# Four graph layers in one launch: the branch and its general arm moved behind the last store, the end of layer 3 rebuilt, three pieces one pair earlier

## The chip, the cores and the metric

The kernel runs on one core of a Trainium2 chip. The metric is the device time of one launch in microseconds (us); less is better. TensorE (PE) multiplies, with its weight loads shown as PEld; VectorE (DVE), ScalarE (ACT) and GpSimd (POOL) work element by element; SyncE (SP) issues most DMAs. Each engine takes its instructions in a fixed order. Between engines there are semaphores.

## The reference

There are 3327 nodes with 64 features each and a weighted, sparse 3327 x 3327 adjacency. Four layers follow each other, each of them `x = layernorm(x + layer(x, adj))`:

```python
# layer 0: mean over neighbours, beside the node itself
neigh = (adj @ x) / (adj.sum(1) + 1);   l0 = concat([x, neigh]) @ W.T
# layer 1: logarithm map between every pair of nodes (Poincare ball), weighted sum, exponential map
log_ij = logmap(x[:, None], x[None, :]); agg = einsum('ij,ijc->ic', adj / deg, log_ij)
l1 = expmap(0, agg @ weight + bias)
# layer 2: neighbours again, relu, each row divided by its norm
z = concat([x, (adj @ x + x) / deg]) @ W + b;  l2 = relu(z) / norm(relu(z))
# layer 3: of each row's neighbours the last 100 count, with weights that halve from the last one back
pos = rank - (deg - k);  w = mask * 0.5 ** (k - pos);  l3 = w @ (x @ weight) + bias
```

The final layernorm's result, 3327 x 64 float32, is the output.

## The kernel before

**Tiling.** The nodes are padded to 3328 = 26 blocks of 128. The columns of the transposed adjacency (the nodes that are being computed) are four chunks of 832; the rows (their neighbours) are 13 pairs of blocks. One load brings one pair for one chunk, 832 KB, into one of four buffers `adjp`. An accumulator is two PSUM banks' worth of half chunks (416 columns). PSUM has three double tiles (`two0` to `two2`, handed out by `banks.pair`) and two single ones (`one0`, `one1`, by `banks.one`).

**Layer 0** takes the chunks in the order 0, 3, 1, 2. It aggregates (L488) and on the way counts each row's neighbours for layer 3 (`count`, L560: rank bytes that ACT stores, L570). After each chunk `sums0` makes the sum of squares of its nodes; `features0`, which makes the layer's output from them, is put beside the next chunk's work, and for the last chunk beside the first steps of layer 1.

**The branch.** Layer 1 has two forms. `layer1_far` uses a short polynomial that is valid when no node lies near the origin of the ball; `layer1_near` is the general form. `sums0` marks near nodes in `near_nodes`; at the end of layer 0 the marks are summed (`nearest`, L796), summed over partitions by a small matmul (L798), and cast to an integer (`n_near`, L799). Each of the five engines loads this integer into a register (L1597) and branches (L1599). The far arm holds layers 1 to 3 in the far form; the near arm, behind it in every engine's program, holds layers 1 to 3 again with the general layer 1. With these inputs the far arm is taken. An instruction of an arm cannot stand ahead of the branch.

**Layer 1, far.** A step is one block of neighbours for one chunk, 104 in all. PE makes an inner product `v` (L858); DVE makes `p` from `v` and the adjacency (L869); ACT and POOL make the factor `s` (L882, L883, L884), or ACT and DVE do (L874, L877); six steps later PE aggregates with `s` (L889). Where an epilogue runs beside the steps, POOL has five of six factors, elsewhere every second one.

**Layer 2** takes the chunks in the order 2, 3, 1, 0: aggregation (L488) and an epilogue (`epilogue2`) that also writes `parts`, the operands of layer 3.

**Layer 3** sums `parts` with weights that are expanded from the rank bytes. A *piece* is one pair of blocks for one chunk. Its weights (`bits`) are made by ACT with an exponential (engine letter S, L1384), or by DVE and POOL (letter G: `exponents`, L1362, then L1380); the letters of the 52 pieces stand in `L3_ENGINES`. The first 18 pieces are put between pairs of layer 2 as `L3_AMONG` says: `{chunk turn: {pair: pieces}}`. Six pieces (`FILL3`, three for each of the chunks 0 and 3) use bf16 parts; the last 16 are the pairs 0 to 3 (`LATE3`) of chunks 2, 1, 0 and 3 in that order (`ORDER3`). Chunks 2 and 1 accumulate in double tiles, chunk 0 in the two single ones, chunk 3 in a double one.

After a chunk's last piece `keep_sums3` copies its two halves to SBUF (L1455), one on DVE and one on ACT. `epilogue3` multiplies with the weight (L1465), adds the residual (`y`, L1472, DVE), squares (L427, ACT), sums (L430, DVE), takes the inverse root of the variance and scales (`o`, L1488), and SP stores. The last chunk does this in two halves of 3 and 4 blocks. For the roots there is `deviation` (eight small DVE steps, L386 to L397) or, once ACT's root table is loaded (L1390, behind the last piece that ACT widens), `table_root` (one ACT lookup, L445, and three small DVE steps, L448 to L450).

The order on each engine is the order in which the code emits the work, changed by a scheduler where an instruction is not ready in its estimate; `issue_after(a, b)` fixes that `a` comes behind `b` on an engine.

Of the kernel before, what the change touches and what calls it, by code (L numbers as in the profile page):

```python
# [20 lines left out]
FP = mybir.dt.float32  # L21
# [5 lines left out]
AF = mybir.ActivationFunctionType  # L27
# [8 lines left out]
D = 64  # L36
# [80 lines left out]
L3_AMONG = {2: {5: 2, 8: 2, 12: 3}, 3: {1: 2, 3: 3, 8: 3, 10: 3}}  # L117


L3_ENGINES = "SSG" * 6 + "GSGSGS" + "S" * 12 + "SG" * 6 + "GSSG"  # L120
# [11 lines left out]
def four_gnn_layers_kernel(  # L132
# [109 lines left out]
    for t, value in ((minus_last, -1.0), (last_bias, 200.0)):  # L242
# [4 lines left out]
        )  # L247

# [430 lines left out]

    with ExitStack() as l0s:  # L680
        banks = Banks(l0s, "l0psum")
# [112 lines left out]
        count(masked, places, 0, counted)  # L794
        nearest = small.tile([P, 1], FP, name="nearest", tag="nearest")
        nc.vector.tensor_reduce(nearest, near, axis=AX.X, op=ALU.add)  # L796
        vote = banks.one(NCH % 2)
        nc.tensor.matmul(vote[0:1, 0:1], lhsT=nearest, rhs=ones, start=True, stop=True)  # L798
        nc.vector.tensor_copy(n_near, vote[0:1, 0:1])  # L799

    setup_stack.close()
# [31 lines left out]
    def layer1_far(banks):  # L845
        with tc.tile_pool(name="l1w", bufs=1) as wp:
# [109 lines left out]
            del work  # L956
            pairs = adj_pairs(first_pairs)
            waiting, last, side, total, summed, kept = [], None, None, NCH * NB, None, {}
            for start in range(0, total + L1_AHEAD, L1_GROUP):
                group = range(start, start + L1_GROUP)  # L960
                made = []
                for i in group:
                    if i < total:
# [5 lines left out]
                        v, v_issued = far_v(c, jb, summed)  # L969
# [3 lines left out]
                for i in group:  # L973
# [21 lines left out]

                    if late is None and i in (late_at, late_at + 2):
                        k0, k1 = (0, 4) if i == late_at else (4, GB)
                        transposes0(ORDER[-1], banks.one(1), v_issued, False, k0, k1)
# [23 lines left out]
            own = banks.pair()[:, 0, :]  # L1022
# [6 lines left out]
    def layer1_near():  # L1029
        with ExitStack() as stack:  # L1030
            all_of(features0(ORDER[-1], *last_group, Work(blocks_of(ORDER[-1])[2])))
            transposes0(ORDER[-1], Banks(stack, "l1b").pair())
# [184 lines left out]
    def begin2(banks, loading, loaded, behind):  # L1217
# [3 lines left out]
        rows = last_rows([(c, rank[:, c]) for c in ORDER2 if c != LATE_RANKS])  # L1221
        next(rows)
# [6 lines left out]
    def layers_2_and_3(banks, acc, done, rows, there):  # L1229


        with tc.tile_pool(name="l2m", bufs=M16) as mp, tc.tile_pool(name="late", bufs=1) as late:
# [86 lines left out]
            summed, split, loaded_all = [], [], []  # L1319
# [13 lines left out]
            def expand(behind=None):  # L1333
# [44 lines left out]
                for t, b in made:  # L1378
# [4 lines left out]
                    else:  # L1383
# [3 lines left out]
                        if k == last_widened and b != 0:  # L1387
                            done = t.bitcast(FP)
                            done = done[:, 1, 0:1] if len(t.shape) == 3 else done[:, 0:1]
                            nc.scalar.activation(nothing, done, AF.Abs_reciprocal_sqrt, bias=1.0)  # L1390
# [5 lines left out]
            def piece(k, behind=None):  # L1396
# [18 lines left out]
                if c not in acc3:  # L1415
                    if c == ORDER3[2]:
# [4 lines left out]
                bits, last = bits_of.pop(k), jp == LATE3[-1]  # L1421
                for b in range(2):
# [36 lines left out]
            def epilogue3(b0, b1_, bank, behind, made):  # L1459
# [11 lines left out]
                y = node_tile("y3")[:, 0:nb, :]  # L1471
# [4 lines left out]
                work = Work(nb)  # L1476
                ss = work("ss")
                held["adj"].append(-1)
                o = adjp.tile([P, 2, CH], FP, name="o", tag="adj").rearrange("p t c -> p (t c)")
# [174 lines left out]
```

## Time and profile before

| what | us |
|---|---|
| three runs | 514.81, 516.00, 516.71; median 516.0 |
| the profiled execution, whole time | 514.87 |
| its span, first to last instruction of the profile | 513.1 |
| so around the span | 1.8 |
| PE busy in the span | 470.9 (92%) |
| DVE, ACT, POOL busy | 388.5, 343.8, 210.0 |
| granted TensorE clock, mean | 0.987 |

The profile is one execution. A line of the timeline gives the start, the duration, the engine, the source line, what was done, and in brackets how long the engine had been idle and what ended that. Merged lines with `x4` run from the first start to the last end of four instructions. In the chain of waits a line gives start, length and what the end of the kernel was then waiting for. The windows view gives the busy time of each engine in a stretch. An engine name with a q (DVEq, SPq) is its sequencer, which loads registers, branches and issues DMAs.

### The profile page before, as it was taken

To read this page: it belongs to the slowest core of one execution; us is meant where nothing else is said; L and a number is where in the kernel's file an instruction comes from. 1 tells how busy PE (TensorE), PEld (TensorE's weight loads), DVE (VectorE), ACT (ScalarE), POOL (GpSimd) and SP (SyncE) were. 2 spreads that over 40 slices of the span, in tenths; PEclk is the share of its full clock that TensorE was granted. 3 is DMA by queue.
4 is the path that set the end of the run, shared out by engine and by line. 5 is a ranking of instruction groups with operands and counts; after the bars stand their busy time and mean duration, and the time that the engine had idled before them with its cause. 6 is when DMAs were issued, how large, how long until landed. Compare 5 with 4: busy or idle time off the path is not lost.

```text
span 513.1 us, 7873 instructions
## 1 busy us (share of the span) xinstructions
PE 470.9 (92%) x2888; PEld 239.7 (47%) x2888; DVE 388.5 (76%) x709; ACT 343.8 (67%) x430; POOL 210.0 (41%) x174
## 2 busy tenths in 40 slices
PE   5999999999966999999999999999999999899892
PEld 3444344454432333443443344354565555367782
DVE  3475429979849989889979987978787687637884
ACT  2445556686768988879968987820378746479862
POOL 2000201102118996769867986800412044310650
PEclk9999999999999999999999999999999999999996
DMA  8899999989729688867876788499779889950002
GB/s 273 293 387 329 391 388 371 320 291 307 264 78 341 220 265 269 256 200 263 265 246 220 243 271 258 164 343 399 264 242 361 294 317 333 303 225 2 0 1 74
DMA packets 46289, 132.49 MB, mean 258 GB/s; under 512 B 7046, under 2 KB 7150, under 8 KB 46178
## 3 DMA queue, kind: packets, MB, share of 16 engines
q1 hardware_dynamic: 45714, 131.36, 74.3%
q0 software_dynamic: 384, 0.52, 0.4%
q8 instruction: 24, 0.39, 0.3%
q14 instruction: 23, 0.19, 0.1%
q10 hardware_dynamic: 144, 0.03, 0.0%
HBM read 130.88 MB, written 0.85 MB: 257 GB/s over the span
## 4 chain that ended last, share of the span: by engine, by line
PE 49%; DVE 23%; DMA 12%; ACT 9%; issue 3%; POOL 2%; SPq 1%; DVEq 0%; POOLq 0%
DMA adj<-in_adjt_dram 12%; PE two L858 12%; PE one L889 11%; PE one L488 11%; PE two L560 4%; DVE mask L546 4%; PE two L488 4%; DVE mask L514 3%; ACT s L882 3%; ACT s L883 2%; DVE p L869 2%; PE two L1439 2%; DVE exponents L1362 2%; DVE s L877 2%; PE two L926 1%
## 5 line engine op out<-in xcount | busy, mean ns | idle before, releaser
L884 POOL TENSOR_TENSOR s<-s,p 128x832 f32<-128x832 f32 x70 | 135.5, 1955 | 34.6 <-DVE p L869 21.1
L869 DVE SCALAR_TENSOR_TENSOR p<-two,adj 128x832 f32<-128x832 f32 x100 | 101.6, 1019 | 15.1 <-issue 11.1
L570 ACT ACTIVATE rank<-two,last_bias 128x832 uint8<-128x832 f32 x78 | 71.8, 951 | 45.5 <-PE two L560 23.0
L858 PE MATMUL two<-uw 64*128 64x416 f32 x416 | 89.7, 544 | 8.7 <-DVE s L877 3.9
L889 PE MATMUL one<-s,xu 128*64 128x416 f32 x416 | 86.1, 525 | 0.0
L488 PE MATMUL one<-adj,x0w 128*64 128x416 f32 x416 | 82.9, 524 | 3.1 <-ACT x0w L698 1.8
L882 ACT ACTIVATE s<-two 128x832 f32<-128x832 f32 x70 | 60.0, 859 | 27.6 <-DVE p L869 27.1
L546 DVE SCALAR_TENSOR_TENSOR mask<-two,minus_last,mask 32x832 bf16<-32x832 f32 x48 | 52.5, 1093 | 30.8 <-PE two L560 27.5
L858 PEld LDWEIGHTS two<-uw 64*128 64x128 f32 x416 | 37.5, 189 | 60.6 <-PE one L889 16.9
L514 DVE TENSOR_SCALAR mask<-adj 128x1664 bf16<-128x1664 f32 x48 | 50.6, 1055 | 19.0 <-DMA adj<-in_adjt_dram 18.3
L883 ACT ACTIVATE s<-s 128x832 f32<-128x832 f32 x70 | 62.6, 897 | 1.8
L560 PE MATMUL two<-mask,tri 128*64 128x416 bf16 x416 | 52.3, 341 | 6.0 <-DVE mask L546 3.8
L488 PE MATMUL one<-adj,xr 128*64 128x416 f32 x264 | 54.1, 518 | 2.8 <-DMA adj<-in_adjt_dram 2.8
L889 PEld LDWEIGHTS one<-s,xu 128*64 128x64 f32 x416 | 26.0, 136 | 48.1 <-issue 41.7
L488 PEld LDWEIGHTS one<-adj,x0w 128*64 128x64 f32 x416 | 28.8, 138 | 35.5 <-issue 23.6
L1384 ACT ACTIVATE bits<-rank 128x832 fp32r<-128x832 uint8 (+1 forms) x42 | 38.8, 985 | 8.0 <-PE two L1439 6.0
L560 PEld LDWEIGHTS <-tri 128*64 128x64 bf16 x416 | 25.6, 110 | 38.4 <-issue 24.1
L1380 POOL TENSOR_SCALAR bits<-exponents 128x832 fp32r<-128x832 bf16 (+1 forms) x21 | 26.0, 1253 | 41.5 <-DVE exponents L1362 20.4
L877 DVE SCALAR_TENSOR_TENSOR s<-two,p 128x832 f32<-128x832 f32 x34 | 34.6, 1017 | 0.8 <-ACT two L874 0.3
L1439 PE MATMUL two<-bits,parts 128*128 128x416 f32 x144 | 30.9, 360 | 2.5 <-POOL bits L1380 2.3
L488 PEld LDWEIGHTS one<-adj,xr 128*64 128x64 f32 x264 | 20.8, 136 | 24.0 <-issue 15.9
L874 ACT ACTIVATE two<-two 128x832 f32<-128x832 f32 x34 | 28.8, 847 | 4.4 <-DVE p L869 3.6
(290 smaller groups left out, 540.3 us busy)
## 6 DMA issues: line engine op xcount, KB each, us to landing
adj<-in_adjt_dram SPq DMA_DIRECT2D x135, 832.0 KB, 5.6
uw<-in_adjt_dram SPq DMA_DIRECT2D x7, 832.0 KB, 6.2
a<-in_adjt_dram SPq DMA_DIRECT2D x8, 416.0 KB, 6.7
sums<-in_adjt_dram SPq DMA_DIRECT2D x2, 832.0 KB
p<-in_adjt_dram SPq DMA_DIRECT2D x4, 416.0 KB, 5.5
s<-in_adjt_dram SPq DMA_DIRECT2D x4, 416.0 KB, 6.8
uw<-in_xt_dram SPq DMA_DIRECT2D x1, 640.0 KB
out_dram<-o SPq DMA_DIRECT2D x2, 192.0 KB, 2.4
```

Of the source, the lines that this page charges most:

```text
L488: issued = nc.tensor.matmul(acc[h * D : (h + 1) * D, 0:HC], lhsT=x[:, 2 * jp + k, 0:D], rhs=a[:, bass.ts(h, HC)], start=(first and k == 1) ...
L514: issued = nc.vector.tensor_scalar(mask, a2, 0.0, None, op0=ALU.not_equal)
L546: ranks.carried = nc.vector.scalar_tensor_tensor(halves(last), ranks.after[P - 32 : P, :, 0:HC], minus_last[P - 32 : P, :], halves(last), ...
L560: issued = nc.tensor.matmul(counts[k][rows, h, 0:HC], lhsT=lhsT[:, rows], rhs=mask[:, of, bass.ts(h, HC)], start=lhsT is tri, stop=(k == 1 ...
L570: ranks.made = nc.scalar.activation(halves(ranks.rank[:, 2 * jp + k, :]), counts[k][:, :, 0:HC], AF.Relu, bias=last_bias,)
L858: issued = nc.tensor.matmul(v[:, h, 0:HC], lhsT=wt[rows, bass.ts(jb, P)], rhs=ut[rows, bass.ds(c * CH + h * HC, HC)], start=True, stop=True,)
L869: issued = nc.vector.scalar_tensor_tensor(halves(p), v, 0.25 - 0.5 * FD, halves(a), op0=ALU.add, op1=ALU.mult)
L877: return nc.vector.scalar_tensor_tensor(halves(s), v, FG, halves(p), op0=ALU.add, op1=ALU.mult)
L882: nc.scalar.activation(halves(s), v, AF.Square, bias=FB - 0.5, scale=-2.0)
L883: nc.scalar.activation(s, s, AF.Copy, bias=FG)
L884: nc.gpsimd.tensor_mul(s, s, p)
L889: issued = nc.tensor.matmul(acc[h * D : (h + 1) * D, 0:HC], lhsT=xu[:, jb, 0:D], rhs=s[:, bass.ts(h, HC)], start=first, stop=last,)
```

## The change

1. The far arm is no longer an arm. Layers 1 to 3 follow layer 0 straight, in the PSUM tiles of layer 0 (one set of `Banks` for all). PE's first `v` is ordered behind the last count.
2. The vote (`nearest`, the small matmul, `n_near`) stands at the end of layer 1, behind its last aggregation, in the second bank of the tile `own`.
3. The branch stands behind everything, as `tc.If(some_near > 0)` without an else. Its arm computes layers 1 to 3 again in the general form and stores over the output. It needs layer 0's output `xr`, which layer 1 overwrites, so POOL's queue writes it to HBM (`kept_x1`, 128 partitions of 6,656 bytes, 832 KB) when its last group is done; the arm reads it back. The arm doesn't repeat layer 3's `last_rows`.
4. In layer 2's last chunk three pieces stand behind pair 7 instead of pair 8.
5. The last piece of layer 3 goes from G to S, and so the table load moves behind this piece.
6. Chunk 3 accumulates in the two single tiles and chunk 0 in the double one; the fill pieces of chunk 3 come first. In chunk 3's last pieces the first half's matmuls end three matmul pairs ahead of the second half's.
7. Layer 3's epilogues of chunks 2, 1 and 0 stop after the sum of squares; their roots are finished later, with an ACT lookup and five small steps and the scaling on POOL. Chunks 2 and 1 are finished beside the last chunk's pieces, chunk 0 between the two halves of chunk 3. Those halves keep `table_root` and the scaling on DVE, in tiles of their own.

The diff, cut to its core:

```diff
-L3_AMONG = {2: {5: 2, 8: 2, 12: 3}, 3: {1: 2, 3: 3, 8: 3, 10: 3}}
+L3_AMONG = {2: {5: 2, 8: 2, 12: 3}, 3: {1: 2, 3: 3, 7: 3, 10: 3}}
-L3_ENGINES = "SSG" * 6 + "GSGSGS" + "S" * 12 + "SG" * 6 + "GSSG"
+L3_ENGINES = "SSG" * 6 + "GSGSGS" + "S" * 12 + "SG" * 6 + "GSSS"
...
+    kept = ctx.enter_context(tc.tile_pool(name="kept", bufs=1, space=bass.MemoryType.DRAM))
+    kept_x1 = kept.tile([P, NB, D], FP, name="kept_x1")
...
+    far = ExitStack()
+    banks = Banks(far, "psum_far")
     with ExitStack() as l0s:
-        banks = Banks(l0s, "l0psum")
...
-        count(masked, places, 0, counted)
+        counted = count(masked, places, 0, counted) or counted
+        banks.turns = [places.turn, 1, 2 - places.turn]
+    setup_stack.close()
+    def vote(bank, behind):
         nearest = small.tile([P, 1], FP, name="nearest", tag="nearest")
         nc.vector.tensor_reduce(nearest, near, axis=AX.X, op=ALU.add)
-        vote = banks.one(NCH % 2)
-        nc.tensor.matmul(vote[0:1, 0:1], lhsT=nearest, rhs=ones, start=True, stop=True)
-        nc.vector.tensor_copy(n_near, vote[0:1, 0:1])
-    setup_stack.close()
+        issue_after(nc.tensor.matmul(bank, lhsT=nearest, rhs=ones, start=True, stop=True), behind)
+        nc.vector.tensor_copy(n_near, bank)
...
-                        v, v_issued = far_v(c, jb, summed)
+                        v, v_issued = far_v(c, jb, summed or ahead_of)
...
+                    if late is None and i == late_at:
+                        nc.gpsimd.dma_start(out=kept_x1, in_=xr)
...
-            own = banks.pair()[:, 0, :]
+            own = banks.pair()
+            vote(own[0:1, 1, 0:1], summed)
+            own = own[:, 0, :]
...
     def layer1_near():
-        with ExitStack() as stack:
-            all_of(features0(ORDER[-1], *last_group, Work(blocks_of(ORDER[-1])[2])))
-            transposes0(ORDER[-1], Banks(stack, "l1b").pair())
+        nc.sync.dma_start(out=xr, in_=kept_x1)
...
-                    if c == ORDER3[2]:
+                    if c == ORDER3[3]:
                         acc3[c] = [banks.one(h) for h in range(2)]
...
+                if c == ORDER3[-1] and jp in LATE3:
+                    to_end.append((c, jp, bits))
+                    if len(to_end) < len(LATE3) - 1:
+                        turns3 = [(0, *to_end[-1]), (1, *to_end[-1])]
+                    elif len(to_end) == len(LATE3) - 1:
+                        turns3 = [(0, *to_end[-1])]
+                    else:
+                        turns3 = [(0, *to_end[-1]), (1, *to_end[-2]), (1, *to_end[-1])]
...
             def epilogue3(c, b0, b1_, bank, behind):
...
+                nc.scalar.activation(sq, y, AF.Square)
                 yield
-                if any(bank is last for c in ORDER3[1:] for last in acc3[c]):
-                    r, k = table_root(ss, work, made[-1]), -0.5 / D
+                nc.vector.tensor_reduce(ss, sq, axis=AX.X, op=ALU.add)
+                yield
+                if not ends_with:
+                    r, h = work("root"), work("part")
+                    issue_after(nc.scalar.activation(
+                        r, ss, AF.Abs_reciprocal_sqrt, bias=ln_eps, scale=1.0 / D
+                    ), tables[0])
+                    nc.gpsimd.tensor_scalar(h, ss, D * LN_EPS, -0.5 / D, op0=ALU.add, op1=ALU.mult)
+                    nc.gpsimd.tensor_mul(h, h, r)
+                    nc.gpsimd.tensor_mul(h, h, r)
+                    nc.gpsimd.tensor_scalar(h, h, 1.5, 1.0, op0=ALU.add, op1=ALU.mult)
+                    nc.gpsimd.tensor_mul(r, h, r)
+                    nc.gpsimd.tensor_tensor(o, y, col(r, nb), op=ALU.mult)
                 else:
-                    r, k = deviation(ss, work), 1.0
+                    r = table_root(ss, work, tables[0])
+                    nc.vector.scalar_tensor_tensor(
+                        o, y, -0.5 / D, col(r, nb), op0=ALU.mult, op1=ALU.mult
+                    )
...
-            pieces += [(c, jp) for c in ORDER3[2:] for jp in FILL3]
+            pieces += [(c, jp) for c in reversed(ORDER3[2:]) for jp in FILL3]
...
+                        for end in ends if tables and n < NCH else ():
+                            all_of(end)
+                        ends = [] if tables and n < NCH else ends
...
+                        if n == NCH:
+                            for turn3 in (1, 0, 2, 1, 0, 2):
+                                next(ends[turn3], None)
...
+    with far:
+        layers_2_and_3(banks, *layer1_far(banks))
     some_near = nc.values_load(n_near[0:1, 0:1], min_val=0, max_val=NP)
-    with tc.If(some_near == 0) as cmp:
-        with ExitStack() as arm:
-            banks = Banks(arm, "psum_far")
-            layers_2_and_3(banks, *layer1_far(banks))
-    with cmp.Else():
+    with tc.If(some_near > 0):
         done = layer1_near()
```

## The prediction

> **What bounds the kernel now.** I read the page first: which engine is full, and where.
>
> ```profile
> PE 470.9 (92%) x2888; PEld 239.7 (47%) x2888; DVE 388.5 (76%) x709; ACT 343.8 (67%) x430; POOL 210.0 (41%) x174
> ```
>
> PE sets the pace over the whole. The windows view says where it does:
>
> ```profile
> 146.00:152.00 6.00, 2.10 (x22) 1.33 (x22) 4.47 (x15) 3.55 (x5) 0.33 (x1) 0.96 0.45 142
> 152.00:174.00 22.00, 17.66 (x80) 6.91 (x80) 18.45 (x35) 17.32 (x22) 19.73 (x16) 0.93 0.88 284
> 186.00:338.00 152.00, 148.87 (x770) 61.96 (x770) 135.05 (x216) 124.11 (x156) 114.06 (x59) 1.00 0.73 241
> 500.00:513.00 13.00, 3.41 (x20) 2.94 (x18) 6.36 (x21) 2.64 (x7) 0.00 (x0) 0.62 0.29 73
> ```
>
> From 186 to 338 PE is full (152 / 770 = 0.197 us a matmul), and the windows up to 463 are nearly as full. So what comes earlier ahead of 186 stays earlier to the end. PE is empty in two places: at the join of layers 0 and 1, and after 500. The chain of waits shows the join:
>
> ```profile
> 150.15 0.18 DVE near_nodes L615
> 150.35 0.19 DVE nearest L796
> 150.58 0.20 PE one L798 x2
> 150.81 0.16 DVE n_near L799
> 150.97 0.99 issue
> 151.96 3.13 PE two L858 x8
> 155.12 1.03 DVE p L869
> ```
>
> The 0.99 us "issue" is the register load (0.48 to 0.54 us on each engine in the rows of the tile `n_near`), the branch and the waits behind it. The timeline of the end shows copies, matmuls and halves one after the other:
>
> ```profile
> 497.06 1.58 POOL L1380 TENSOR_SCALAR bits<-exponents 128x1664 fp32r<-128x1664 bf16 x1 [1.70 <-DVE part L391]
> ...
> 500.63 0.58 DVE L1455 COPY sums<-two 128x416 f32<-128x416 f32 x1
> ...
> 501.25 0.51 ACT L1455 COPY sums<-two 128x416 f32<-128x416 f32 x1 [2.90 <-DVE sums L1455]
> ...
> 503.20 1.97 PE L1465 MATMUL two<-w3s,sums 128*128 128x64 f32 x8 [0.52 <-DVE y L1472]
> ...
> 507.97 0.42 DVE L1488 SCALAR_TENSOR_TENSOR o<-y,root 128x256 f32<-128x256 f32 x1
> ```
>
> **The join: -3.6 us.** Without the vote DVE is done with `sums0` at 150.33 (150.15 + 0.17) and goes on to `p`, which now starts at 153.92. PE ends its last count at 147.99 and ACT its last rank store at 149.58, so the first two `v` are there before DVE is free. 153.92 - 150.33 = 3.6. The second pair of adjacency landed at 151.35 and is asked for two `p` later, at 152.4; SP can issue the third and later pairs from 147.2 instead of 151.71. At most PE's own lead counts, 151.96 - 147.99 = 4.0; at least 2.4, if DVE has to wait for ACT's last rank store and one full `v` and `p` (149.58 + 1.9 against 153.92). I take 3.6, since DVE is the last to come free.
>
> **`kept_x1`: +0.3.** One DMA issue on POOL. No transfer of 128 partitions from POOL is in the trace; its issues cost 0.51 (L585) to 1.77 us (L591, mean). POOL is full in 174 to 186 (12.00 of 12.00), but PE is too, and behind 186 POOL has 25% to spare. So 0 to 1.8, taken 0.3. Queued behind it on POOL are layer 1's factors. The 832 KB are one load more among 135; the DMA share is 0.81 in 174 to 186. SP's queue isn't passed.
>
> **The vote: +0.3.** A reduce of 0.18 and a cast of 0.15 on DVE, a matmul of 0.2 on PE at about 338.9, where own products (1.7 us) cover the copies of `sums`. Should the reduce stand behind the two L903 products (they end at 340.88) and the matmul ahead of the own products, PE waits 2.0 and the 28 matmuls behind it with it. 0 to 2.2; the reduce's input is ready since layer 0, so near the low end.
>
> **Three pieces a pair sooner: -1.4.** The row that carries it:
>
> ```profile
> 449.10 1.62 PE L488 MATMUL one<-adj,xr 128*64 128x416 f32 x8 [2.03 <-DMA adj<-in_adjt_dram]
> ```
>
> PE stands 2.03 us for pair 8's load. The three pieces (12 matmuls, 2.44 us) take that wait; their last weights were there at 446.79 (ACT, 445.90 + 0.89). Pair 8 then starts at 449.5, pairs 9 and 10 landed at 451.17 and 452.19, pairs 11 and 12 at 455.4 and 457.5 (+0.3, as pair 8's buffer comes free later). Pairs 9 and 10, the transposes (0.9), the next three pieces (2.4) and the last two pairs (3.0) end at 460.7 instead of 462.36, 1.6 sooner; 1.4 for small gaps. Behind it stands DVE's chain to `parts` (12.4 us, to 477.3), which starts everything after 478. At least 0, if weights come late, at most 2.0.
>
> **Layer 3's end: -2.4.** POOL's last weights end at 498.64 and PE's last piece at 499.72. As S the piece takes ACT 1.6 us (0.80 a half) behind its other weights (495.11), a square of 0.51 between: 497.2. But chunk 0's second copy and its 14 matmuls (1.8 us) wait in the same stretch, and then eight matmuls of pieces (1.4 to 2.1 us), so I leave PE's end at 499.7, -0.7 to +1.3. From there to DVE's last `o` it is 8.67 us now. With single tiles the copies stand side by side (0.63 instead of 2.0 us up to 501.76), DVE has no roots of other chunks ahead of its copy, and the second half's matmuls don't wait for `y`: 0.63 + 0.9 + 1.0 (matmuls of both halves) + 0.42 (`y`) + 0.42 (square) + 0.42 (sum) + 0.30 (root) + 0.6 (three steps) + 0.42 (`o`) + 0.24 (gaps) + 0.2 (chunk 0's `y` and sum between) = 5.6. That is -3.1. Against it: POOL's roots stand beside DVE. This row is the price:
>
> ```profile
> 157.93 1.94 DVE L436 SCALAR_TENSOR_TENSOR var<-ss_last,ln_eps 128x7 f32<-128x7 f32 x1
> ```
>
> A step that takes 0.17 us elsewhere took 1.94 beside POOL's L884 (157.91 to 159.86) and ended with it. Steps with an operand in PSUM (L374, 0.16) were not held. DVE's `part`, `root` and `o` lie wholly in SBUF; POOL's widest new operation is the scaling, 0.82 to 0.95 us (128x378 to 128x441). One such hold or several short ones: +0.7, from 0 to 2.9 (three scalings). Sum -2.4, from -4 to +1.
>
> The Trainium skill ("SBUF — State Buffer", Who interferes with whom) speaks here against the change: a VectorE instruction with two inputs in SBUF and a GpSimd instruction that reads SBUF cannot run together, and whichever starts first keeps the other out for its whole length. By that rule all three scalings could hold the last chain and the end would be worth -0.2 instead of -2.4; by the row it is only as much as happens to meet.
>
> **Costed at nothing:** the order of the fill pieces and the tiles that chunks 0 and 3 exchange. The matmuls are the same, and PE has them from 464.87 to 481.4 under DVE's chain to `parts`. If that cover went, the double tile, which DVE's epilogue leaves at 466.25, could hold chunk 0's fills for 1 us at most.
>
> **The branch at the end: +0.5.** SP's final stretch now: last store issued at 508.92, landed at 512.1, barrier to 513.06. Each engine already takes one far branch there: from its branch to its next instruction ACT needs 2.86 us (506.80 to 509.66), DVE 3.00 (507.98 to 510.98), SP 0.50. New is the register load, 0.54 on DVE: 511.5, still ahead of the landing. If SP must wait for its stores before the skipped arm and only then goes through its twelve final waits (0.06 each, 0.75), it costs 0.75 to 1.7. A second far branch would cost 3.0 on DVE, 2.4 of it visible. So 0 to 2.5; I take 0.5, as SP's row has 2.3 us of slack.
>
> **Sum.** -3.6 + 0.3 + 0.3 - 1.4 - 2.4 + 0.5 = -6.3. The profiled execution took 514.87 (span 513.1 and 1.8 around), which gives 508.6. It lies 1.1 under the median of the runs, so the forecast for the median is 516.0 - 6.3 = 509.7.
>
> **Rivals.**
> *The end gives nothing.* POOL holds DVE as in L436's row or ACT's longer row of weights, copies and roots delays chunk 0's copy. Then the end is worth +0.5 instead of -2.4: 512.6. For it: ACT's second copies waited 6.8 us in all for DVE's. Against: of these waits the last is removed by the single tiles.
> *The join was hidden.* In 152 to 174 POOL is 19.73 of 22 us busy, so the ramp has a limit of its own, and if POOL's extra DMA costs its 1.8 there and DMA or ACT hold the first steps, only 1 of 3.6 is left: 513.8, no change that can be told. Against: POOL's first factor (157.91) itself waits for the first `p`.
> *POOL's small steps set the end; slower.* POOL makes fifteen small steps and three scalings in a row, from about 498.0 (table load behind the last weights) minus the 5 gained: 493. No small two-operand step of POOL is in the trace. The line through 128x378 (0.818) and 128x441 (0.923) leaves 0.19 for none; the nearest row itself is 0.82, or 1.35 beside DVE (L612). With 0.2 each the three chunks take 5.9 and end at 499, ahead of DVE's end at 501.6 (508.4 - 3.6 + 0.6 - 1.4 - 2.4). From 0.4 a step they decide; at 1.2 each (18 + 2.9 us) chunk 0's store is issued at 514, and with 3.7 to land, 0.9 of barrier, 1.8 around and the median's 1.1 it is 521.5: slower. I take 0.2 from the line, since memsets of few elements take 0.09.
> *The end is worth all of its copies.* No hold, PE's end 0.7 sooner, no cost at the branch: 507.4.
>
> **How the numbers follow.** Forecast 0.60 (its own range 508.0 to 512.0), the end gives nothing 0.14, join hidden 0.08, POOL sets the end 0.10, the full end 0.08. The range 507.0 to 513.8 leaves out the slow case and the edges. About 0.5% (2.6 us) is what a measurement of this kernel can tell from no change, so faster means under 513.4: 0.60 + 0.12 + 0.08 = 0.80. Within it are the hidden join and the weak part of "gives nothing", 0.10; slower 0.10.
>
> **What would show it.** First `p` at 150.4 and layer 1's last aggregation at about 335.5 (338.9 now); no wait for a load at pair 8; chunk 3's two copies side by side; from PE's last piece to the last `o` 5.6 to 6.3 us instead of 8.7; POOL's small steps at 0.2 us; DVE's small steps at 0.17 unless POOL runs; between the last store's landing and the end at most 1.5 us. The forecast is wrong if `p` doesn't move, if POOL's scaling of chunk 0 ends behind DVE's last `o`, or if SP still works through waits long after the last landing.

## The result and the profile after

The changed kernel took 518.3 us (median of 22 runs, 515.3 to 522.5) against 515.4 us of the kernel before on the same chip: ratio 1.006, 95% interval 1.0037 to 1.0082. It is slower by about 3.1 us, where 6.3 us less was forecast, and it lies outside the range of 507.0 to 513.8. The profiled run happens to be its quickest (515.31 us, span 513.5); a second profile, further down, has a span of 517.5, nearer to the median.

The engines' line of the page and the windows that answer to those of before (columns: window, its length, busy us and count for PE, PEld, DVE, ACT and POOL, granted clock, DMA share, GB/s):

```profile
PE 473.0 (92%) x2888; PEld 239.9 (47%) x2888; DVE 381.6 (74%) x690; ACT 345.5 (67%) x432; POOL 215.2 (42%) x192
```

```profile
146.00:152.00 6.00, 5.34 (x47) 3.20 (x46) 3.76 (x10) 5.92 (x9) 0.00 (x0) 1.00 0.78 249
152.00:174.00 22.00, 17.09 (x82) 5.75 (x80) 19.88 (x42) 18.92 (x23) 17.04 (x11) 1.00 0.50 169
186.00:338.00 152.00, 148.20 (x768) 61.62 (x766) 134.71 (x213) 124.52 (x156) 114.24 (x59) 1.00 0.74 240
500.00:513.00 13.00, 3.32 (x28) 3.07 (x27) 5.15 (x15) 3.24 (x11) 4.99 (x16) 0.70 0.31 74
```

PE is no longer empty from 146 to 152, but not because layer 1 starts sooner: layer 0 ends later. Its last count ends at 152.07 (147.99 before). The join is 4.5 us shorter (first `p` 1.39 us after the last count instead of 5.93), so the first `p` comes at 153.46, 0.46 us sooner than before, and layer 1's last aggregation 0.8 us later than before. The rows, first of the kernel before, then of the changed one, where DVE takes the first `p` even ahead of the sum (L433) that belongs to `sums0`:

```profile
147.45 0.54 PE L560 MATMUL two<-mask,minus 128*64 128x416 bf16 x4
153.92 1.02 DVE L869 SCALAR_TENSOR_TENSOR p<-two,sums 128x832 f32<-128x832 f32 x1 [2.96 <-PE two L858]
```

```profile
151.53 0.54 PE L563 MATMUL two<-mask,minus 128*64 128x416 bf16 x4
153.46 1.02 DVE L866 SCALAR_TENSOR_TENSOR p<-two,sums 128x832 f32<-128x832 f32 x1
154.40 0.60 DVE L433 TENSOR_REDUCE ss_last<-sq 128x7 f32<-128x441 f32 x1
```

The join's gain is there; layer 0 had lost as much ahead of it. The timeline of GpSimd's queue shows what is new in layer 0, first of the changed kernel at its start:

```profile
4.19 0.79 POOL L585 MEMSET last_more<- 78x832 uint8 x1
4.92 0.09 POOL L727 MEMSET wl<- 1x1 f32 x1
4.96 1.75 POOL L587 DMA_DIRECT2D last_a<-in_adjt_dram  x3
```

and of the kernel before, where the same instructions stood behind the branch:

```profile
151.67 0.79 POOL L582 MEMSET last_more<- 78x832 uint8 x1 [20.88 <-DVE n_near L799]
152.41 0.73 POOL L584 DMA_DIRECT2D last_a<-in_adjt_dram  x1
153.14 0.51 POOL L585 DMA_DIRECT2D last_more<-rank  x1
```

Nothing in `last_rows` changed. But the three loads of `last_a` wait for no result, and with the branch gone nothing kept them back; the planner put them at 4.96 us. The DMA view of 2 to 20 us shows what they meet, first of the kernel before, then of the changed one (queue, packets, MB, share of the 16 engines):

```profile
q1 hardware_dynamic: 2312, 6.08, 99.8%
```

```profile
q1 hardware_dynamic: 1604, 5.39, 94.7%
q0 software_dynamic: 96, 0.26, 5.1%
```

SP's queue was full before (99.8%) and moves 0.69 MB less beside GpSimd's 0.26 MB. At 340 GB/s, the mean of that window before, 0.69 MB are 2.0 us, and DVE's fourth mask stands 1.9 us later (timelines of DVE, before and after):

```profile
16.03 1.03 DVE L514 TENSOR_SCALAR mask<-adj 128x1664 bf16<-128x1664 f32 x1 [0.51 <-DMA adj<-in_adjt_dram]
```

```profile
17.94 1.03 DVE L517 TENSOR_SCALAR mask<-adj 128x1664 bf16<-128x1664 f32 x1 [1.61 <-DMA adj<-in_adjt_dram]
```

In this profile PE then ran at half the clock from 20.6 to 27.5 us, and the 1.9 us had become 4.1 by the thirteenth mask. The windows of 20 to 42 us, before and after (the third number from the end is the clock):

```profile
20.00:42.00 22.00, 20.95 (x150) 10.66 (x148) 13.94 (x30) 9.14 (x13) 0.14 (x1) 1.00 0.93 329
```

```profile
20.00:42.00 22.00, 19.89 (x120) 9.87 (x122) 12.03 (x28) 9.33 (x13) 0.00 (x0) 0.84 0.88 290
```

The second new wait is at the vote. The changed kernel's timeline behind layer 1's last aggregation:

```profile
339.67 0.19 PE L809 MATMUL two<-ones,nearest 128*1 128x1 f32 x2
339.94 0.62 DVE L840 TENSOR_TENSOR xr<-one,vn 128x441 f32<-128x441 f32 x1
340.48 0.13 DVE L810 CAST n_near<-two 1x1 int32<-1x1 f32 x1
340.67 1.77 PE L909 MATMUL two<-w1r,uw 64*128 64x64 f32 x14 [0.81 <-DVE n_near L810]
```

The vote's result lies in the second half of the pair that the own products (L909) write. They wait for DVE's cast, and the cast waits behind `xr`: 0.81 us, with the matmul 1.0.

The pieces behind pair 7 do what was forecast. The wait for pair 8's load (2.03 us before) is gone; what is left is 0.32 us at pair 7:

```profile
448.00 1.62 PE L491 MATMUL one<-adj,xr 128*64 128x416 f32 x8 [0.32 <-DMA adj<-in_adjt_dram]
449.55 2.52 PE L1465 MATMUL two<-bits,parts 128*128 128x416 f32 x12
452.00 3.21 PE L491 MATMUL one<-adj,xr 128*64 128x416 f32 x16
```

The end, too, is much as forecast. Chunk 3's copies no longer wait for each other (DVE 499.73, ACT 501.66, each right behind its own half), GpSimd's small steps take 0.20 us, and from PE's last piece (501.62) to DVE's last `o` (507.03) it is 5.4 us, 8.7 before:

```profile
499.73 0.59 DVE L1481 COPY sums<-one 128x416 f32<-128x416 f32 x1 [2.24 <-PE one L1437]
501.19 0.43 PE L1437 MATMUL one<-bits,parts 128*128 128x416 f32 x1
501.66 0.51 ACT L1481 COPY sums<-one 128x416 f32<-128x416 f32 x1 [0.98 <-PE one L1437]
506.61 0.42 DVE L1541 SCALAR_TENSOR_TENSOR o<-sq,a 128x256 f32<-128x256 f32 x1
```

One DVE step met GpSimd's scaling of chunk 0:

```profile
505.42 0.94 POOL L1538 TENSOR_TENSOR o<-twice,root 128x448 f32<-128x448 f32 x1
505.48 0.89 DVE L452 TENSOR_TENSOR var<-var,a 128x4 f32<-128x4 f32 x1
506.41 0.16 DVE L453 SCALAR_TENSOR_TENSOR a<-var,a 128x4 f32<-128x4 f32 x1
```

A step of 0.16 us took 0.89: a hold of 0.73, as priced (0.7). Then the tail: from the last `o` to the end 6.5 us instead of 4.7.

### The profile page after: what moved, and what is told of

Read it like the earlier page. It is cut to its first block, busy times and chain, and to the rows that moved or that the text cites. A ratio compares the mean times of both kernels' runs of the same rounds, so it can differ in the third digit from the quotient of the medians.

```text
span 513.5 us, 7874 instructions
## 1 busy us (share of the span) xinstructions
PE 473.0 (92%) x2888; PEld 239.9 (47%) x2888; DVE 381.6 (74%) x690; ACT 345.5 (67%) x432; POOL 215.2 (42%) x192
## 4 chain that ended last, share of the span: by engine, by line
PE 53%; DVE 23%; DMA 9%; ACT 7%; issue 5%; POOL 2%; SPq 1%; POOLq 0%; DVEq 0%; ACTq 0%
PE one L491 14%; PE two L855 10%; PE one L886 9%; DMA adj<-in_adjt_dram 8%; PE two L563 5%; DVE p L866 4%; DVE mask L549 4%; PE two L491 4%; PE two L1465 3%; DVE mask L517 3%; ACT s L879 3%; DVE s L874 2%; ACT s L880 2%; DVE exponents L1364 2%; PE two L923 1%
## 5 line engine op out<-in xcount | busy, mean ns | idle before, releaser
L491 PE MATMUL one<-adj,x0w 128*64 128x416 f32 x416 | 85.3, 539 | 4.0 <-ACT x0w L702 2.6
L855 PEld LDWEIGHTS two<-uw 64*128 64x128 f32 x416 | 36.1, 185 | 61.8 <-issue 27.6
L563 PE MATMUL two<-mask,tri 128*64 128x416 bf16 x416 | 53.6, 346 | 5.6 <-DVE mask L549 3.9
L491 PE MATMUL one<-adj,xr 128*64 128x416 f32 x264 | 55.7, 518 | 0.8 <-DMA adj<-in_adjt_dram 0.8
L491 PEld LDWEIGHTS one<-adj,x0w 128*64 128x64 f32 x416 | 29.9, 142 | 37.3 <-issue 25.7
L1382 POOL TENSOR_SCALAR bits<-exponents 128x832 fp32r<-128x832 bf16 (+1 forms) x20 | 24.4, 1237 | 36.5 <-PE one L1465 19.3
L573 ACT ACTIVATE uw<-two,last_bias 128x832 uint8<-128x832 f32 x26 | 24.0, 951 | 12.2 <-DVE mask L549 6.1
```

The source lines that it names most:

```text
L491: issued = nc.tensor.matmul(acc[h * D : (h + 1) * D, 0:HC], lhsT=x[:, 2 * jp + k, 0:D], rhs=a[:, bass.ts(h, HC)], start=(first and k == 1) ...
L563: issued = nc.tensor.matmul(counts[k][rows, h, 0:HC], lhsT=lhsT[:, rows], rhs=mask[:, of, bass.ts(h, HC)], start=lhsT is tri, stop=(k == 1 ...
L573: ranks.made = nc.scalar.activation(halves(ranks.rank[:, 2 * jp + k, :]), counts[k][:, :, 0:HC], AF.Relu, bias=last_bias,)
L855: issued = nc.tensor.matmul(v[:, h, 0:HC], lhsT=wt[rows, bass.ts(jb, P)], rhs=ut[rows, bass.ds(c * CH + h * HC, HC)], start=True, stop=True,)
```

## The experiments

All ratios are to the kernel before, measured beside it; 0.001 is 0.52 us.

| kernel | median us | ratio (95% interval) | us |
|---|---|---|---|
| changed | 518.3 | 1.006 (1.0037 to 1.0082) | +3.1 |
| e1 changed, loads held | 515.6 | 1.0002 (0.9976 to 1.0027) | +0.1 |
| e2 before, loads early | 519.8 | 1.0084 (1.0061 to 1.0108) | +4.3 |
| e3 changed, no general arm | 517.2 | 1.003 (1.0003 to 1.0057) | +1.5 |
| e4 before, new end | 512.8 | 0.9964 (0.9939 to 0.9989) | -1.9 |
| e5 e1 and own bank | 511.3 | 0.9914 (0.9883 to 0.9945) | -4.4 |
| e6 e5 and chunk 0's store on ACT | 510.8 | 0.9902 (0.9874 to 0.9931) | -5.0 |
| e7 e4 and the pieces sooner | 512.3 | 0.994 (0.992 to 0.996) | -3.1 |
| e8 before, mended join alone | 514.1 | 0.9979 (0.9956 to 1.0002) | -1.1 |
| e9 e5 with the changed kernel's order | 513.8 | 0.9949 (0.9917 to 0.9981) | -2.6 |
| e10 changed, own bank alone | 514.2 | 0.9984 (0.9953 to 1.0015) | -0.8 |
| e11 e6 without the store of x1 | 510.4 | 0.9888 (0.9845 to 0.993) | -5.8 |
| e12 changed again | 518.6 | 1.0047 (1.0005 to 1.0089) | +2.4 |

**e1: the loads held.**

```
-        nc.gpsimd.memset(more, 200.0)
+        issued = [nc.gpsimd.memset(more, 200.0)]
...      (the loads of a and more are appended to issued)
+        for load in issued if hold is not None else ():
+            issue_after(load, hold)      # hold: layer 0's last count
```

> The changed kernel with the four kinds of GpSimd work of `last_rows` (the memset of `last_more`, the three loads of `last_a`, the three of `last_more`) put in GpSimd's order behind layer 0's last count, where the branch kept them before. Theory A (these loads, hoisted to 4.2 to 7 us, collide with the first adjacency loads): the fourth mask of layer 0 is back at about 16.0 us (17.9 in the changed kernel), layer 0's last count at about 148.0 (152.1), the first `p` at about 149.5 to 150.3 (153.5), and the time falls by 3 to 4.5 us, from 518.3 (median of the changed kernel) to 514 or less; against the kernel before 0.990 to 0.998. Rival B (layer 0 is late because of the clock, or because the new DRAM tile and the longer life of the PSUM pool moved something else): mask four and last count stay at 17.9 and 152, the time stays at 515 to 518. Rival C (the start is back, but the gain is given back at the join because GpSimd's loads now stand in the ramp): last count 148, first `p` 150, but the aggregation of layer 1 ends as late as now (339.7), time 517 to 518.

Measured: fourth mask 16.36, last count 147.28, first `p` 148.68, layer 1's last aggregation 334.96, 4.0 us sooner than before and within 0.6 of the prediction's 335.5. The edit orders the planner's list and makes no engine wait: in the profile the memset stands at 130.0 us and the first load at 131.6, the others behind the last count. So the loads are out of layer 0's start. Theory A holds for layer 0, and the time fell by 3.0 us, though to 515.6 and a ratio of 1.0002, not to the 514 or less that it asked for. And the lead was gone at the end of layer 2 (3.3 us later than before). So a second loss lies between 335 and 466 us.

**e2: the loads early in the kernel before.**

```
-            nc.gpsimd.dma_start(out=a[k * NB : (k + 1) * NB, :], in_=adjt[c, :, P - 1, :])
+            if len(chunks) == 1:
+                nc.gpsimd.dma_start(out=a[k * NB : (k + 1) * NB, :], in_=adjt[c, :, P - 1, :])
...
+    for k, c in enumerate(c for c in ORDER2 if c != LATE_RANKS):     # ahead of layer 0
+        nc.gpsimd.dma_start(out=last_a[k * NB : (k + 1) * NB, :], in_=adjt[c, :, P - 1, :])
```

> The kernel before with one thing added: the three loads of `last_a` for layer 2 are asked for on GpSimd's queue ahead of layer 0's first step instead of behind the branch; all else, the branch and the join too, is left. Theory A: layer 0's fourth mask at about 17.9 instead of 16.0 us, the last count at 150 to 152 instead of 148.0, and the time rises by 2 to 4.5 us, ratio 1.004 to 1.009. Rival B: nothing moves in layer 0, ratio 0.998 to 1.002 (the three loads that no longer stand behind the branch are worth under 1 us there, since GpSimd waits for the first `p`).

Measured: +4.3 us, theory A. With no other part of the change, the fourth mask stands at 18.14 and the last count at 149.88. The DMA view of 2 to 20 us is that of the changed kernel:

```profile
q1 hardware_dynamic: 1593, 5.36, 95.1%
q0 software_dynamic: 96, 0.26, 5.2%
```

Over all profiles, the last count ends at 151.1 us on average in the five with early loads (149.9 to 152.6) and at 148.0 in the nine others (147.2 to 149.4): 3.1 us, about what e1 gave back. Not all of e2's 4.3 us is lost in layer 0. In its profile the lag is 1.9 us from the first `p` to layer 1's last aggregation, 3.6 behind a half-clock window at 344.4 us, and 4.9 at layer 2's end. How much of that the loads set off and how much is the clock's spread is not shown.

**e3: no general arm.**

```
-    some_near = nc.values_load(n_near[0:1, 0:1], min_val=0, max_val=NP)
-    with tc.If(some_near > 0):
...
```

> The changed kernel without the register load, the branch and the general arm behind it (left out: the computation for near pairs, which these inputs do not need); the vote itself stays. Theory (the skipped arm makes SP wait for its stores queue by queue before the program's last waits): from DVE's last `o` to the end of the span 4.7 to 5.2 us instead of 6.4, time 1.2 to 1.8 us less than the changed kernel, 516.5 to 517.1. Rival (the tail is set by the order of the stores on SP behind GpSimd's chunk alone): the tail stays above 6 us and the time within 0.5 us of the changed kernel. Layer 0 should stay as late as in the changed kernel (fourth mask 17.9, last count 152).

Measured: 1.5 us less by the ratios, as expected; tail 5.56 us, more than the 4.7 to 5.2 expected; layer 0 as late as expected (18.98 and 152.64). Over all profiles the time from the end of the last store's issue to the end of the span is 3.8 to 4.1 us in the five that have no skipped arm there, and 4.5 to 5.0 in the seven that have one and keep all stores on SP. The arm costs 0.8 us in the tail: SP's twelve last waits (0.06 each) now begin only when the last store has landed. The rest of the tail is another matter, see e4 and e6.

**e4: the end alone.** The diff is that of the change for layer 3, without `L3_AMONG`, in the kernel before.

> The kernel before with the new end of layer 3 alone: the fill pieces in reversed order, the one-bank tiles for chunk 3, the last piece by ACT, GpSimd's roots for three chunks and the two halves side by side; the join, the branch and the pieces among pairs of layer 2 are as before. Theory (the profile of the changed kernel: DVE's last `o` came 2.7 us nearer to the end of layer 2, and the stores then went out behind GpSimd's chunk 0): last `o` 2.3 to 3.0 us sooner than before, end of span 1.7 to 2.7 us sooner, time 512.7 to 513.8, ratio 0.994 to 0.998. Rival (GpSimd's roots or the stores' order eat it all): ratio 0.999 to 1.003.

Measured: -1.9 us (interval -0.6 to -3.1), as expected. DVE's last `o` came 2.3 us sooner, but the tail is 6.4 us here too, with the branch at its old place. The rows of SP's stores say why: four stores now fall within 3 us, and the issue of one took 1.62 us instead of 0.37. In the profiles of e5, e7, e9, e10 and e12 one took 1.55 to 2.02. In the profile of before no store took more than 0.45. It does not happen every time: in the first profile of the changed kernel none took more than 0.48. There the tail's 1.8 us are 0.55 of later issue (three stores instead of two come behind the last `o`) and 1.2 behind the last issue, with the arm in it.

**e5: the vote in a bank of its own**, on top of e1.

```
-            own = banks.pair()
-            vote(own[0:1, 1, 0:1], summed)
-            own = own[:, 0, :]
+            own = banks.pair()[:, 0, :]
+            vote(banks.one(NCH % 2)[0:1, 0:1], summed)
```

> The first experiment's kernel (loads held behind layer 0) with the vote's matmul in a PSUM bank of its own instead of the second half of the own products' pair. With it the planner's order of DVE in layer 2's second chunk is again that of the kernel before. Theory A: no 0.81 us wait of PE for `n_near`; from layer 1's last aggregation to layer 2's first 3.4 to 3.7 us (4.3 in the changed kernel, 3.3 before), the 2.75 us or so that the second chunk of layer 2 lost between 384 and 398 us falls to that of before; together 1.6 to 2.2 us less than the first experiment, 513.3 to 514. Theory B (the clock gate: after short idle times of PE whole windows of 3.4 us run at half the clock, 1.7 us of matmul time each; the first experiment had one pair of them at 337.3 right behind the wait for the vote and one at 432.9): with the waits gone the median of the granted clock rises to 0.986 or more and the time falls by 3 us or more, 512.5 or less. Rival C: neither matters, 515 to 516.

Measured: 4.5 us less than e1 by the ratios, well over the 1.6 to 2.2 of theory A. Its timeline:

```profile
337.46 0.19 PE L809 MATMUL one<-ones,nearest 128*1 128x1 f32 x2
337.58 0.43 PE L909 MATMUL two<-w1r,uw 64*128 64x64 f32 x2
337.91 0.14 DVE L810 CAST n_near<-one 1x1 int32<-1x1 f32 x1
337.94 1.78 PE L923 MATMUL two<-wl,sums 128*128 128x66 f32 x14
```

The vote now stands among the own products and nobody waits for the cast. The time is in theory B's range (512.5 or less), but its sign, a higher clock, is missing: the median is 0.985 in e1 and 0.9845 here. So neither theory is right as it stands. What did change besides the wait is the order that the planner gives DVE in layer 2 from 384 to 398 us; e9 takes that alone.

**e9: that order alone.**

```
                         x2, based = prologue2(c, issued)
+                        if n == 1:
+                            issue_after(summed[-1], based)
```

> The kernel of the run with the own bank (511.3) with one order added: DVE's sum `ss` of layer 2's first chunk is put behind `twice` of the second chunk's `prologue2`, which gives DVE between 384 and 398 us the order of the changed kernel, with no wait for the vote. Theory A (of the 4.2 us between the first experiment and the run with the own bank, the larger part is this order: PE waits 1.4 to 1.9 us for `sums` ahead of the second chunk's `wl` products where the others wait 0 to 0.6, and the ranks' tail is later): 512.3 to 514.0, 1 to 2.7 us more than with the own bank, PE's wait for `sums` back at 1.2 us or more. Rival B (the order costs nothing that lasts; the difference is the wait for the vote and half-clock windows that it sets off): 511.0 to 511.8.

Measured: 1.8 us more than e5 by the ratios, 2.4 by the medians; the intervals of the two overlap. The order is nearly that of the changed kernel (`ss` stands behind the last step of `twice`, there behind the first). The wait is there. PE's waits from 380 to 437 us, in the changed kernel:

```profile
PE two L1269 <- DVE sums L474: 1.4, 1, 1.4
```

and from 330 to 437 us in e9 and e12 alike:

```profile
PE two L1269 <- DVE sums L474: 1.9, 1, 1.9
```

Before, it was 0.6 us (L1267), e6 and e11 have 0.3 and 0.7, and e5, e8 and e10 show no such line. In e9's profile the lead over the kernel before is 2.1 us at layer 2's 312th aggregation matmul of 416 and a lag of 2.2 at the 320th. Not all of these 4.3 us belong to the order: beside the wait for `sums` PE waits 1.1 us for `parts`, and a half-clock window (430.5 to 433.9 us) falls there. The first profile of the changed kernel, without such a window, loses 0.7 between the same two matmuls. So e9 shows that the order brings the wait; the 1.8 us are its price only in part. In this order DVE takes `ss` of the first chunk behind `twice` of the second, and the root, `xu`, `parts` and the last masks of the ranks follow later: in the changed kernel's profile `xu` and `parts` by 2.8 us and the last masks by 1.0 to 1.9, counted against the masks ahead of them.

**e10: the own bank alone.**

> The changed kernel with the vote in a bank of its own and nothing else changed; the early loads of `last_rows` stay. If the two causes add: 518.3 - 4.2 = 514.1, from 513.4 to 515, layer 0 still late (last count 150 to 152.6). If the bank's effect was an accident of the first experiment's planning: 516.5 to 518.

Measured (the edit of e5 on the changed kernel): 514.2 us, 3.9 us less than the changed kernel by the ratios. The two causes add: 3.0 (loads) and 3.9 (bank) make 6.9, and e5, with both mended, lies 7.5 below the changed kernel.

**e6: chunk 0's store on ACT's queue**, on top of e5.

```
+                if c == ORDER3[2]:
+                    yield
-                nc.sync.dma_start(
+                stored = (nc.scalar if c == ORDER3[2] else nc.sync).dma_start(
...
+                if c == ORDER3[2]:
+                    issue_after(stored, tables[-1])      # DVE's last o
```

> The same with one more change: the store of chunk 0 (GpSimd's) goes out on ScalarE's queue behind ScalarE's last root, so that SP's stores of the last chunk do not stand behind it. Theory: SP's last store is issued 0.5 us after DVE's last `o` instead of 1.1, the end of the span 5.6 to 6.0 us after the last `o` (6.4 in the changed kernel), 0.4 to 0.8 us less than the run with the own bank; 512.6 to 513.5, under the kernel before. Rival: ScalarE, later at its far branch by the store (2.7 us from branch to the next instruction), ends the program: tail 6.4 or more, no gain.

Measured: 0.6 us less than e5, less than the intervals can tell. The half of the expectation about the issue holds, the half about the tail does not. SP's last store is issued 0.46 us after the last `o`, and none takes long, but the tail is 6.8 us: it lands later, 4.6 us after its issue (3.2 before). The rival's reason doesn't hold either: ScalarE is through with its waits at 508.0 us, SP with the last store at 508.8. With this the kernel is faster than the kernel before and the changed one, 0.9902 (0.9874 to 0.9931).

**e7: end and pieces**, without the rest (`3: {1: 2, 3: 3, 7: 3, 10: 3}` in e4).

> The kernel before with the new end of layer 3 and the three pieces a pair sooner, the join and the branch as before: the fourth experiment plus the pieces. Theory: the pieces are worth 1.2 to 1.4 us as the profile of the changed kernel has it (pair 8 waits 0.5 instead of 2.0 us for its load), 511.4 to 511.6 where the end alone had 512.8; ratio 0.991 to 0.994. Rival: the wait for the loads comes back two pairs later and the gain is under 0.4.

Measured: 1.2 us less than e4 by the ratios, 0.5 by the medians. From the end of pair 7 to layer 2's end its profile takes 13.9 us, that of before 15.3 and that of the changed kernel 14.1; neither waits at pair 8.

**e8: the mended join alone**, layer 3's end and the pieces as before, loads held, own bank.

> The kernel before with the new join alone: branch and general arm behind the last store, `kept_x1`, the vote behind layer 1 in a bank of its own, `last_rows`' loads held behind layer 0's last count; layer 3's end and the pieces as before. Theory A (the join's gain holds): the first `p` at 148.7 to 149.5, layer 1's last aggregation 3.7 to 4.2 us sooner than before (338.95), layer 2's end 3 us or more sooner, the tail 0.9 us longer: 512.5 to 513.2, ratio 0.993 to 0.996. Rival B (the join's idle time was a rest that the clock gate gave back elsewhere, or layer 2's loads, at 0.9 to 1.0 of the DMA engines' time from 335 to 360 us, set the pace there): layer 1 ends 4 us sooner, but layer 2 at most 1.5 us sooner, time 514.5 to 516, ratio 0.998 to 1.001.

Measured: -1.1 us (interval -2.3 to +0.1), between the two theories. In its profile the first `p` follows the last count by 1.40 us (5.93 before). The last count itself stands 1.1 us later, so the lead is 3.4 us at the first `p`; 2.1 of it are left at layer 1's end, 2.6 at layer 2's, and 1.9 at the end of the span.

**e11: no store of x1** (the saved x1 for the general arm is left out).

> The kernel with all mended (510.8) without the store of `kept_x1` (the saved x1 for the general arm is left out; these inputs do not read it). The prediction set +0.3 for it, within 0 to 1.8. If it is 0.3 or less: 510.2 to 511.0, and layer 1's ramp loses 0.5 to 0.7 us of the join's lead between the first `p` and the 52nd aggregation as with the store. If the store is what takes the ramp's lead: 509.5 or less and the lead at the 52nd aggregation is within 0.2 us of that at the first `p`.

Measured: 0.4 us less by the medians, 0.7 by the ratios, within what the intervals leave open. The lead shrinks from 4.9 us (first `p`) to 4.3 (52nd of layer 1's 416 aggregation matmuls) without the store too (4.6 to 4.0 with it), so the ramp's loss is not the store's.

**e12: the changed kernel again.**

> The changed kernel again, for a second profile beside its fastest one. Expected: 517.5 to 519; layer 0's fourth mask at 17.9 to 19.0 us and its last count 1.9 to 4.7 us behind that of before (1.9 if no window of half clock falls into the start, 4 or more if one or two do); PE's wait for the vote 0.8 us; PE's wait for `sums` ahead of the second chunk's products 1.2 to 1.9 us; and one or two more windows of half clock than the first profile.

Measured: 518.6 us; fourth mask 18.28 us, last count 1.9 us late with no half-clock window at the start, the vote's wait 0.8 us, the wait for `sums` 1.9 us. Not as expected, the half-clock windows are not more than in the first profile: two, now at 340.8 us, where they cost 3.3 us (from layer 1's last aggregation to layer 2's 52nd the lag grows by 4.3 us, in the first profile by 1.0). And one store's issue took 2.02 us, for a tail of 7.7 us (6.5 in the first profile).

## Why the prediction was wrong, point by point

**The join, -3.6: the gain is there, the step was not complete.** The first `p` moved to within 1.4 us of the last count, 5.9 before. That is 4.5 us, more than the 4.0 given at most, since the sum assumed that `p` comes behind all of `sums0`. With the loads held it stands at 148.6 to 150.8, where 150.3 was forecast. The step that failed is its list of what can move ahead once the branch is gone: it asked what SP can issue sooner (pairs 3 and later) and what PE and DVE can start, but not GpSimd. A branch holds back every instruction behind it on every engine. The prediction quoted GpSimd's row of loads (L585, 0.51 us) as a price and did not ask where the loads go. They went 147 us ahead, into a stretch in which SP's queue was 99.8% of the DMA engines' time. Cost: 3.0 us in e1's return, 4.3 in e2; directly seen are the 1.9 us of the fourth mask.

**The vote, +0.3: mis-sized, 3.9.** The prediction weighed one bad case, the reduce behind L903, with 2.0 us. The wait came by another way: the tile. The diff puts the vote into the pair of the own products, so the work named as its cover waits for it. The profile shows 1.0 us for this. e9 puts 1.8 us more on the order of DVE in layer 2, which the planner chose once the vote stood there; that price is uncertain, as said at e9. Where the remaining 1.1 us go stays open. The median clock is 0.982 in the changed kernel and 0.9845 in e10, by estimate 1.3 us of 515, so they may lie in the clock.

**"What comes earlier ahead of 186 stays earlier to the end": too strong.** It holds roughly: of e1's and e6's lead at the first `p` (5.2 and 4.6) 4.0 and 3.4 are left at layer 1's end. The losses are short, counted in layer 1's 416 aggregation matmuls: 0.6 to 0.7 us up to the 52nd (1.8 in e5, with a half-clock stretch from 155.6 us), then 0.35 us between the 104th and 156th in every kernel with the new join, and 0.2 between the 260th and 312th in all of them but e11, which has no store of x1. Join, vote, store and branch were to give -2.5 together; e8 measured -1.1.

**Three pieces a pair sooner, -1.4: about right** (-1.2 by the ratios of e7 and e4, whose intervals overlap; 1.4 and 1.2 behind pair 7 in the profiles of e7 and of the changed kernel).

**Layer 3's end, -2.4: right in mechanism and near in size** (-1.9, e4). The steps of its sum show in the timeline: copies that don't wait for each other, one hold of 0.73 us, small steps of 0.20 us. The rival in which GpSimd's small steps set the end falls by that 0.20. The cost was in what the prediction placed under the branch: the stores crowd on SP.

On the skill's rule there ("SBUF — State Buffer", Who interferes with whom): of GpSimd's three scalings only the last was running when a DVE step with two SBUF inputs was due, and it held that step to its end (to 506.38 against 506.36), as the rule has it. DVE's reductions and its steps with a PSUM operand ran at 0.34 to 0.62 us beside the other two.

**The branch at the end, +0.5:** 0.8 in the tails of the profiles, its low case of 0.75. Unforeseen was the issue of 1.5 to 2.0 us among crowded stores.

**The sum.** Forecast -6.3, measured +3.1; no rival named either of the two causes. Of the 9.4 us, 3.0 are the loads, 3.9 the vote's bank (e10), 1.4 the join with the store, the branch and the mended vote (e8 against -2.5), 0.5 the end and 0.2 the pieces; 0.4 are left, less than the intervals. Mended in these two places the kernel takes 511.3 (e5), -4.4 us, inside the range that was given for the change.

## What to carry to other kernels

A branch, or any barrier, is also a fence for work that depends on nothing: before taking one out, list every instruction behind it, engine by engine, that has no producer (memsets, loads), and ask into which stretch it will rise; if that stretch is bound by the same resource, tie it down. A result of one element costs its wait, not its size: look at which tile it lands in, and who writes the rest of that tile next. When a small wait is added under a planner, the order of later work can change too, so compare the engines' order well past the edit.

## What the runs showed of the hardware

From 2 to 20 us 0.26 MB of GpSimd's loads displaced 0.69 MB on SP's queue, with the DMA engines at 1.01 of their time in both (340 and 316 GB/s); why more than byte for byte is open.

Stores in quick succession on one queue: 0.37 us an issue becomes 1.55 to 2.02 for one of them in the profiles of e4, e5, e7, e9, e10 and e12, not in those of the changed kernel, e1 and e3 (0.48 to 0.63 at most).

Half-clock stretches of 3.41 us, or 6.83, fall into full stretches of PE. The windows of e6, the middle one cut at the clock's own edges:

```profile
335.70:339.18 3.48, 3.48 (x30) 3.25 (x30) 1.83 (x5) 0.94 (x2) 0.00 (x0) 1.00 1.02 397
339.18:342.59 3.41, 3.41 (x11) 1.24 (x12) 2.85 (x6) 0.15 (x1) 0.00 (x0) 0.50 1.03 413
342.59:346.00 3.41, 3.41 (x22) 1.41 (x20) 2.37 (x12) 0.60 (x2) 0.00 (x0) 1.00 1.03 405
```

Eleven matmuls instead of 22 in the middle one, so 1.7 us lost, although PE was busy for all of the window ahead of it, with 64- and 66-column matmuls. e1, e5, e11 and e12 have such a window near there, and so does e2 with the old join; the profile of before and the first of the changed kernel have none, with the same matmuls. "TensorE: Matmul & The Clock Gate" of the Trainium skill (Part 1) gives windows of about 3.4 us that run free of the kernel's start, and half the clock after an idle one. The lengths agree with the rows; "idle" does not, since no idle time is seen ahead of e6's. In columns, though, that window is thin: 28 matmuls of 64 or 66 columns are 1,820, against 22 x 416 = 9,152 in the window behind; whether the clock's control takes that for idle was not tested.

One such window is 0.0033 of the span's mean clock. The kernels' medians differ by about that: 0.979 in e2, 0.982 in the changed kernel, 0.983 before (35 runs), 0.985 in e1, 0.9845 in e5, 0.9885 in e6. So some of what the loads and the vote cost may come by way of such windows. No run here holds the clock fixed, so that share stays open.
